# Normalizing and turning a batch's activations with ScalarE and DMA in place of VectorE and TensorE, with the first gate reordered

## The chip, the cores and the metric

The kernel runs on one core of a Trainium2 chip. The time is the device time of one execution in microseconds (us). The kernel before was timed three times ahead of the prediction: 1895.6 us in the median, 1895.07 to 1895.95.

## The reference, cut to what matters

There are 64 graphs of 256 nodes with 256 channels, in f32. One layer is applied to each:

```python
h = jnp.maximum(_layernorm(x, axis=-1), 0.0)          # "h" below, turned: channels on partitions
# inside the layer, with x = h:
xc = jnp.transpose(x, (0, 2, 1))
h = relu(bn1(conv1(xc)))                               # 256 -> 256, one tap
h = bn2(conv2(h))                                      # 256 -> 256, 17 taps
x_conv = jnp.transpose(relu(h + xc), (0, 2, 1))
s = x @ w_se.T + b_se                                  # 3 numbers per node
A = jnp.exp(-dist(s)) * mask                           # mask = adj
msg = relu(x @ w_msg.T + b_msg)
x_nmp = jnp.einsum('bnm,bmd->bnd', A, msg)
gi = concat([x_conv, x_nmp]) @ w_ih.T + b_ih           # GRU gate
gh = x @ w_hh.T + b_hh
... r, z, n as in a GRU ...
return (1.0 - z) * nn_ + z * x                         # added to the layer's input
```

## The kernel before

Two graphs make a pair (512 columns), four pairs make a block of eight graphs. There are 32 pairs and eight blocks. conv2 is done by a transform along the nodes: 16 "bins" of products with transformed weights (`wb`, read from DRAM again in each block), then back transforms on VectorE (DVE) and ScalarE (ACT). While block b is worked on, the pairs `nxt` to `nxt+3` of block b+1 are loaded, normalized, turned and put through conv1. In the trace the tiles are called `x` (a loaded pair), `hT` (turned h), `h` (conv1's result), `zT` (the three numbers for the distances), `e` (Exp of the distances), `Yv` (conv2's result), `halves` (16-bit halves, turned by DMA), `halves_d` (the same in DRAM).

In the timelines read here, the order of instructions on each engine is that of the program text. A `pace` object only postpones DVE's transform steps; `pace.flush(mark)` issues all postponed steps up to a mark.

```python
def load_x(i, eng=nc.sync):                       # SyncE's queue
    X[i] = work.tile([P, G * MC, D], FP, name="x", bufs=2)
    load_rows(X[i], x, i, eng)

def turn_adj(i):                                  # the adjacency is turned by DMA already
    HALVES[i] = late.tile([P, 2 * MC, W], U16, name="halves")
    nc.sync.dma_start_transpose(out=HALVES[i],
                                in_=adj[G * i:G * (i + 1)].rearrange("g n m -> (g n) m").bitcast(U16))

def keep_adj(i):                                  # and put away in DRAM
    ADJD[i] = dram.tile([L // 2, 2 * MC, NW, W], U16, name="halves_d", bufs=6)
    v = ADJD[i].rearrange("h q (k a) n -> k a (h q) n", a=4)
    for k in range(2 * MC):
        nc.sync.dma_start(out=v[k], in_=HALVES[i][:, k])

# norm_steps: DVE takes means and variances, GpSimd the power, then DVE scales:
def scale(j):
    nc.vector.tensor_scalar(X[i][:, j, :], X[i][:, j, :], t["mv"][:, j, 0:1], t["rstd"][:, j:j + 1],
                            ALU.subtract, ALU.mult)

def transpose_h(i):                               # eight TensorE transposes per pair
    HT[i] = work.tile([P, DC, W], FP, name="hT", bufs=6)
    for dc in range(DC):
        p = aux()
        for j in range(G * MC):
            transpose(chunk(p, j // MC, j % MC), X[i][:, j, dc * P:(dc + 1) * P])
        ...
            nc.scalar.activation(HT[i][:, dc, :], p, AF.Relu)
    if i + 2 < B // G:
        load_x(i + 2)

def gates(i, dc, wait=None, early=None):          # h, xn: early products; xc: conv2's
    ...
    product(ghn, h, n, True, True)
    nc.scalar.activation(gn, ghn, AF.Identity, ...)
    product(pr, h + xn, r, True, False)
    if early:
        early()
    product(pn, xn, n, True, False)
    product(pz, h + xn, z, True, False)
    if wait:
        wait()
    product(pr, xc, r, False, True)               # xc is Yv: conv2's result after its Relu
    nc.scalar.activation(tr, pr, AF.Tanh, ...)
    ...

# the middle of a block:
products(b, 6)                # bins 12 and 13; each bin loads the weights of the bin three later
transpose_h(nxt)
products(b, 7)                # bins 14 and 15
...
aggregate(i + 1)
message(i + 2)
conv1(nxt)
embed(i + 2)
def wait(j=0):
    pace.flush(joined[j])
gates(i, 0, wait, lambda i=i: affinity(i + 2, True))     # affinity: the distances and their Exp
load_adj(i + 3)
turn_adj(nxt)
gates(i, 1)
...
```

## Time and profile before

| | before |
|---|---|
| median of the first three runs | 1895.6 us |
| span of the profiled run | 1898.5 us |
| steady block, start to start | 221.6 us |
| TensorE's mean granted clock, as a share of the full one | 0.989 |

The prediction below shows the lines of the page and reads them; here is only how they are written. A line of a timeline has a start, a duration, an engine, a source line, an operation, `out<-in`, shapes and a count, and in brackets how long the engine stood idle just before and what released it. PE is TensorE, SPq is SyncE's DMA-issuing queue. The durations of TensorE's instructions overlap (a product of 512 columns lasts 594 ns on the page, and the next starts after 0.43 us), so a steady loss on TensorE is counted from the start of one product to the start of the next, less the usual distance of such products (0.43 us for 512 columns, 0.11 us for 128). "Stop" below means that excess at one place.

### The profile page before, as it was taken

What the parts mean: (1) busy time and instruction counts of PE and PEld (TensorE: products, weight loads), DVE (VectorE), ACT (ScalarE), POOL (GpSimd) and SP (SyncE); (2) the same over time, 40 slices, a digit from 0 to 9 for tenths busy, and PEclk for the clock granted to TensorE, in tenths of its full rate; (3) what the DMA queues carried; (4) which work ended last, traced back from release to release, by engine and by line L of the source; (5) the groups of instructions that cost most, each with busy time, mean ns of one, the idle gap of its engine ahead of it and who ended that gap; (6) DMA issues with size and microseconds to landing.
All of it is one profiled execution on the core that took longest, in us unless ns stands there. A gap on an engine that the chain in (4) does not pass through costs nothing.

```text
span 1898.5 us, 21985 instructions
## 1 busy us (share of the span) xinstructions
PE 1836.8 (97%) x7710; PEld 1141.9 (60%) x7710; DVE 1398.1 (74%) x2675; ACT 637.4 (34%) x1335; POOL 206.4 (11%) x324
## 2 busy tenths in 40 slices
PE   6899899999999999999999999999999999999997
PEld 4677445875549554694458755495546944586543
DVE  5778647996399955998379963999559983798522
ACT  2424322243313443235222433134432352224311
POOL 2110110101110110111101011101101111010000
PEclk9989999999999999999999999999999999999999
DMA  5777431672327432492316713274323923063010
GB/s 173 248 241 204 95 82 34 186 186 49 85 55 232 118 87 58 104 244 57 90 34 185 188 48 87 55 229 121 84 61 102 241 62 79 23 182 107 1 44 22
DMA packets 179071, 217.63 MB, mean 115 GB/s; under 512 B 85038, under 2 KB 104778, under 8 KB 178961
## 3 DMA queue, kind: packets, MB, share of 16 engines
q1 hardware_dynamic: 146389, 157.61, 29.1%
q0 software_dynamic: 30464, 56.73, 12.4%
q10 hardware_dynamic: 2108, 1.89, 0.3%
q8 instruction: 61, 1.00, 0.2%
q14 instruction: 49, 0.40, 0.1%
HBM read 156.54 MB, written 44.30 MB: 106 GB/s over the span
## 4 chain that ended last, share of the span: by engine, by line
PE 82%; DVE 8%; DMA 4%; issue 3%; ACT 1%; POOL 1%; ACTq 0%; POOLq 0%; SPq 0%; DVEq 0%
PE acc L479 70%; PE aux L479 8%; PE aux L483 3%; DVE Yv L59 1%; PE aux L759 1%; DMA taps<-in_c_wT_dram 1%; DVE e L766 1%; DVE Yv L62 1%; DVE T L65 1%; DVE Yv L65 1%; DMA wb<-filt 1%; DMA x<-in_x_dram 1%; DMA filt<-fo 1%; DVE msg L731 1%; DVE V L65 1%
## 5 line engine op out<-in xcount | busy, mean ns | idle before, releaser
L479 PE MATMUL acc<-hT,w_hh 128*128 128x512 f32 x768 | 354.5, 598 | 5.0 <-ACT h L618 5.0
L479 PE MATMUL acc<-xnm,w_ih 128*128 128x512 f32 x768 | 353.3, 594 | 0.0
L479 PE MATMUL acc<-Yv,w_ih 128*128 128x512 f32 x768 | 341.1, 594 | 9.5 <-ACT Yv L719 9.5
L479 PEld LDWEIGHTS acc<-Yv,w_ih 128*128 128x128 f32 x768 | 145.4, 190 | 196.0 <-issue 177.0
L479 PEld LDWEIGHTS acc<-xnm,w_ih 128*128 128x128 f32 x768 | 145.9, 191 | 183.3 <-issue 181.3
L479 PEld LDWEIGHTS acc<-hT,w_hh 128*128 128x128 f32 x768 | 144.0, 192 | 172.8 <-issue 161.6
L820 ACT ACTIVATE tr<-acc,b_rz 128x512 f32<-128x512 f32 x64 | 44.0, 687 | 541.6 <-PE acc L479 541.6
L822 DVE SCALAR_TENSOR_TENSOR gn<-tr,gn 128x512 f32<-128x512 f32 x64 | 44.2, 691 | 209.9 <-ACT tr L820 209.9
L848 POOL DMA_DIRECT2D out_dram<-y x64 | 39.0, 615 | 890.9 <-DVE y L847 861.8
L479 PE MATMUL acc<-hT,w_c 128*128 128x512 f32 x256 | 119.9, 613 | 6.4 <-ACT hT L599 5.5
L479 PE MATMUL acc<-U,wb 128*128 128x128 f32 x1024 | 124.8, 276 | 1.1 <-DMA wb<-filt 1.1
L479 PE MATMUL acc<-V,wb 128*128 128x128 f32 x1024 | 124.8, 275 | 0.0
L479 PEld LDWEIGHTS acc<-U,wb 128*128 128x128 f32 x1024 | 120.5, 192 | 5.0 <-DVE Yv L59 2.3
L59 DVE SCALAR_TENSOR_TENSOR V<-T,V 128x256 f32<-128x256 f32 (+2 forms) x224 | 121.6, 609 | 0.3
L479 PEld LDWEIGHTS acc<-V,wb 128*128 128x128 f32 x1024 | 119.5, 192 | 0.0
L479 PE MATMUL aux<-e,msg 128*128 128x256 f32 x464 | 105.0, 380 | 0.0
L479 PEld LDWEIGHTS aux<-e,msg 128*128 128x128 f32 x464 | 86.2, 191 | 11.3 <-issue 1.0
L479 PE MATMUL aux<-w_msg,hT 128*128 128x259 f32 x384 | 92.1, 390 | 0.0
L847 DVE TENSOR_TENSOR y<-aux,y 128x512 f32<-128x512 f32 x64 | 41.1, 684 | 68.4 <-PE aux L483 68.4
L523 POOL TENSOR_TENSOR rstd<-rstd,neg_half 128x4 f32<-128x4 f32 x32 | 36.3, 1134 | 497.2 <-DVE rstd L522 497.1
L65 DVE TENSOR_TENSOR V<-h 128x512 f32<-128x512 f32 x64 | 43.9, 685 | 57.9 <-ACT h L618 57.9
L479 PEld LDWEIGHTS acc<-hT,w_c 128*128 128x128 f32 x256 | 50.0, 197 | 57.7 <-issue 47.3
(148 smaller groups left out, 2737.5 us busy)
## 6 DMA issues: line engine op xcount, KB each, us to landing
wb<-filt SPq DMA_DIRECT2D x376, 256.0 KB
x<-in_x_dram SPq DMA_DIRECT2D x64, 256.0 KB
y<-in_x_dram POOLq DMA_DIRECT2D x64, 256.0 KB, 5.5
out_dram<-y POOLq DMA_DIRECT2D x64, 256.0 KB, 5.2
halves_d<-halves SPq DMA_DIRECT2D x116, 128.0 KB
adjh<-halves_d POOLq DMA_DIRECT2D x116, 128.0 KB, 5.5
filt<-fo SPq DMA_DIRECT2D x24, 252.0 KB
filt<-fo POOLq DMA_DIRECT2D x12, 252.0 KB, 5.3
```

What stands on the lines that cost most here:

```text
L59: return self.step(out, lambda: self.v.scalar_tensor_tensor(out, x, s, y, op0=ALU.mult, op1=ALU.add))
L62: return self.step(out, lambda: self.v.tensor_add(out, x, y))
L65: return self.step(out, lambda: self.v.tensor_sub(out, x, y))
L479: nc.tensor.matmul(p, w, v, **kw)
L483: nc.tensor.transpose(p, v, ident)
L523: nc.gpsimd.tensor_tensor(t["rstd"], t["rstd"], neg_half, ALU.pow)
L731: nc.vector.tensor_add(MSG[i][:, g, c, :], p[:, :D + SE], b_msg)
L759: nc.tensor.matmul(p[:, :N], ZT[rows_q, :P], ZT[rows_q, P:], start=True, stop=True)
L820: nc.scalar.activation(tr, pr, AF.Tanh, bias=b_rz[:, dc:dc + 1], scale=0.5)
L822: nc.vector.scalar_tensor_tensor(gn, tr, 1.0, gn, op0=ALU.add, op1=ALU.mult)
L847: nc.vector.tensor_add(row_tile(Y[i], g), p, row_tile(Y[i], g))
L848: nc.gpsimd.dma_start(out=rows(out, G * i + g), in_=row_tile(Y[i], g))
```

## The change

The intent is to take the transposes of h off TensorE, which is the bound, for 28 of the 32 pairs. ScalarE normalizes a pair in place (Relu with a scale and a shift), a DMA transposes its 16-bit halves from SBUF to SBUF, eight DMAs sort the rows into `hh`, and two ScalarE copies join the halves to `hT`. In the first gate of a block, the distances and conv1 of pair nxt are moved behind the early products, just ahead of the products that need conv2's result.

```diff
+    def turn_h(i):
+        for j in range(G * MC):
+            nc.scalar.activation(X[i][:, j, :], X[i][:, j, :], AF.Relu, scale=STATS[i]["rstd"][:, j:j + 1],
+                                 bias=STATS[i]["shift"][:, j:j + 1])
+        t = late.tile([P, 2 * MC, W], U16, name="halves")          # the adjacency's one buffer
+        TURNED[i] = t.rearrange("p a b -> p (a b)").rearrange("p (q n) -> p q n", n=P)
+        nc.sync.dma_start_transpose(out=TURNED[i], in_=X[i].rearrange("p q d -> p (q d)").bitcast(U16))
+        if i + 2 < B // G:
+            load_x(i + 2)
+    def sort_h(i):
+        HH[i] = late.tile([P, 2 * MC, W], U16, name="hh")
+        for j in range(2):
+            for k in range(K):
+                h = k % 2 * (P // 2)
+                nc.sync.dma_start(out=HH[i][h:h + P // 2, k // 2 * 2 + j, :], in_=TURNED[i][j::2, k::K, :])
+    def join_h(i):
+        HT[i] = work.tile([P, DC, W], FP, name="hT", bufs=6)
+        for j in range(2):
+            nc.scalar.copy(v[:, j], u[:, j])
...
-        norm(nxt)
+        turn_h(nxt)
         affinity(i + 1)
         products(b, 6)
-        transpose_h(nxt)
+        sort_h(nxt)
         products(b, 7)
-        pace.add(mix(fft.p_back(Yu, T), fft.q_factors(Yu)))
+        pace.add(mix(fft.p_back(Yu, T), fft.q_factors(Yu)), scaled)
...
         message(i + 2)
-        conv1(nxt)
-        embed(i + 2)
-        def wait(j=0):
-            pace.flush(joined[j])
-        gates(i, 0, wait, lambda i=i: affinity(i + 2, True))
+        def wait():
+            pace.flush(scaled)
+            join_h(nxt)
+            affinity(i + 2, True)
+            conv1(nxt)
+            pace.flush(joined[0])
+        gates(i, 0, wait, lambda i=i: embed(i + 2))
         load_adj(i + 3)
+        pace.flush(normed[1])
+        turn_h(nxt + 1)
+        sort_h(nxt + 1)
         turn_adj(nxt)
...
-        gates(i, 1)
         keep_adj(nxt)
+        gates(i, 1, None, lambda nxt=nxt: join_h(nxt + 1))
+        pace.flush(normed[2])
+        turn_h(nxt + 2)
+        sort_h(nxt + 2)
         turn_adj(nxt + 1)
-        transpose_h(nxt + 1)
+        keep_adj(nxt + 1)
...                                              (the same for nxt + 2 and nxt + 3 further on)
-        gates(i + 1, 0)
+        gates(i + 1, 0, None, lambda nxt=nxt: join_h(nxt + 2))
         message(i + 3)
         conv1(nxt + 2)
...                                              (y with one buffer, a "shift" per pair; join_adj moved)
```

The checks for pairs beyond the last are left out here. `K` is 4, and `u` and `v` are views of `hh` and `hT`.

More of the change, by code (lines that the diff above doesn't have):

```diff
@@ L425, in load_y @@
     def load_y(i):
-        Y[i] = late.tile([P, G * MC, D], FP, name="y", bufs=2)
+        Y[i] = late.tile([P, G * MC, D], FP, name="y")
         load_rows(Y[i], x, i, nc.gpsimd)
@@ L503, in columns @@
         return [c[:, sum(n[:j]):sum(n[:j + 1])] for j in range(len(n))]
+    STATS = {}
     def norm_steps(i):
@@ L514, in stats @@
                 t["st"] = work.tile([P, G * MC, 6], FP, name="st")
-                t["mv"] = work.tile([P, G * MC, 2], FP, name="mv")
-                t["rstd"] = work.tile([P, G * MC], FP, name="rstd")
+                t["mv"] = work.tile([P, G * MC, 2], FP, name="mv", bufs=2)
+                t["rstd"] = work.tile([P, G * MC], FP, name="rstd", bufs=2)
+                t["shift"] = work.tile([P, G * MC], FP, name="shift", bufs=2)
+                STATS[i] = t
             nc.vector.bn_stats(t["st"][:, j, :], X[i][:, j, :])
@@ L523, in aggregate_stats @@
             nc.gpsimd.tensor_tensor(t["rstd"], t["rstd"], neg_half, ALU.pow)
+            if i >= PB:
+                nc.vector.tensor_scalar(t["shift"], t["mv"][:, :, 0], -1.0, None, ALU.mult)
+                nc.gpsimd.tensor_tensor(t["shift"], t["shift"], t["rstd"], ALU.mult)
         def scale(j):
@@ L601, in transpose_h @@
             load_x(i + 2)
+    TURNED, HH = {}, {}
+    def turn_h(i):
+        if i >= B // G:
+            return
+        for j in range(G * MC):
[7 more added lines that the diff above has]
+    def sort_h(i):
+        if i >= B // G:
+            return
+        HH[i] = late.tile([P, 2 * MC, W], U16, name="hh")
+        K = D * 2 // P
+        for j in range(2):
[3 more added lines that the diff above has]
+    def join_h(i):
+        if i >= B // G:
+            return
+        HT[i] = work.tile([P, DC, W], FP, name="hT", bufs=6)
+        v = HT[i].bitcast(U16).rearrange("p c (n j) -> p j c n", j=2)
+        u = HH[i].rearrange("p (c j) n -> p j c n", j=2)
+        for j in range(2):
+            nc.scalar.copy(v[:, j], u[:, j])
     def conv1(i):
@@ L789, in aggregate @@
             nc.scalar.activation(XNM[i][:, dc, :], p, AF.Copy)
-        join_adj(i + 1)
     OT = {}
@@ L848, in finish @@
             nc.gpsimd.dma_start(out=rows(out, G * i + g), in_=row_tile(Y[i], g))
-        if i + 2 < B // G:
-            load_y(i + 2)
+        if i + 1 < B // G:
+            load_y(i + 1)
     def mix(a, b):
@@ L860, in mix @@
         return q
-    odd, even, normed, halved = (Mark() for _ in range(4))
+    odd, even, halved, scaled = (Mark() for _ in range(4))
+    normed = [Mark() for _ in range(PB)]
     joined = [Mark() for _ in range(PB)]
@@ L937 @@
         pace.flush(even)
+        run(norm_steps(nxt)[0])
         pace.add(fft.branch_back(Yv, T, 2))
@@ L940 @@
         aggregate(i)
-        if b == 0:
+        if b > 0:
+            join_adj(i + 1)
+        else:
             nc.gpsimd.dma_start(out=w_hh, in_=hh_wT.rearrange("(k p) o -> p k o", p=P))
@@ L961, in join @@
             pace.add([(W, lambda o=o: residual(i + j, o)) for o in range(DC)], joined[j])
-        stats, scale = norm_steps(nxt + 1)
         join(0)
-        pace.add(stats)
+        pace.add(norm_steps(nxt + 1)[0], normed[1])
         join(1)
-        pace.add(scale, normed)
         pace.add(split_steps(nxt), halved)
+        pace.add(norm_steps(nxt + 2)[0], normed[2])
         join(2)
@@ L973 @@
         aggregate(i + 1)
+        if b > 0:
+            join_adj(i + 2)
         message(i + 2)
-        conv1(nxt)
-        embed(i + 2)
-        def wait(j=0):
-            pace.flush(joined[j])
-        gates(i, 0, wait, lambda i=i: affinity(i + 2, True))
+        def wait():
[5 more added lines that the diff above has]
+        gates(i, 0, wait, lambda i=i: embed(i + 2))
         if b == 0:
             transpose_a(i + 2)
+            load_y(0)
         load_adj(i + 3)
+        pace.flush(normed[1])
+        turn_h(nxt + 1)
+        sort_h(nxt + 1)
         turn_adj(nxt)
-        if b == 0:
-            load_y(0)
-            load_y(1)
-        gates(i, 1)
         keep_adj(nxt)
+        gates(i, 1, None, lambda nxt=nxt: join_h(nxt + 1))
+        pace.flush(normed[2])
+        turn_h(nxt + 2)
+        sort_h(nxt + 2)
         turn_adj(nxt + 1)
-        pace.flush(normed)
-        transpose_h(nxt + 1)
+        keep_adj(nxt + 1)
         aggregate(i + 2)
+        join_adj(i + 3)
         pace.flush(halved)
         conv1(nxt + 1)
-        stats, scale = norm_steps(nxt + 2)
-        pace.add(stats)
+        pace.add(norm_steps(nxt + 3)[0], normed[3])
         pace.add(split_steps(nxt + 1), halved)
-        pace.add(scale, normed)
         pace.flush(joined[1])
-        gates(i + 1, 0)
-        keep_adj(nxt + 1)
-        turn_adj(nxt + 2)
-        pace.flush(normed)
-        transpose_h(nxt + 2)
+        gates(i + 1, 0, None, lambda nxt=nxt: join_h(nxt + 2))
         message(i + 3)
         conv1(nxt + 2)
-        stats, scale = norm_steps(nxt + 3)
-        pace.add(stats)
         pace.add(split_steps(nxt + 2), halved)
-        pace.add(scale, normed)
         finish(i)
         embed(i + 3)
+        pace.flush(normed[3])
+        turn_h(nxt + 3)
+        sort_h(nxt + 3)
+        turn_adj(nxt + 2)
+        keep_adj(nxt + 2)
         gates(i + 1, 1)
-        keep_adj(nxt + 2)
-        turn_adj(nxt + 3)
         affinity(i + 3)
         load_adj(nxt)
-        gates(i + 2, 0)
+        gates(i + 2, 0, None, lambda nxt=nxt: join_h(nxt + 3))
+        turn_adj(nxt + 3)
         keep_adj(nxt + 3)
-        pace.flush(normed)
-        transpose_h(nxt + 3)
         aggregate(i + 3)
+        join_adj(nxt)
         conv1(nxt + 3)
```

## The prediction

> **What bounds the kernel now.** I read the head of the page first, then the table of stretches (busy time per engine between given times), then the timeline of one block of eight graphs, then the waits of TensorE and of the DMA-issuing queue.
>
> ```profile
> span 1898.5 us, 21985 instructions
> PE 1836.8 (97%) x7710; PEld 1141.9 (60%) x7710; DVE 1398.1 (74%) x2675; ACT 637.4 (34%) x1335; POOL 206.4 (11%) x324
> PE   6899899999999999999999999999999999999997
> PEclk9989999999999999999999999999999999999999
> ```
>
> TensorE is busy from the third slice on, at full clock. The stretches show the same by block: the kernel is 107 us of set-up, then eight blocks; the steady ones repeat every 221.6 us.
>
> ```profile
> core 0: us, PE busy (x) PEld busy (x) DVE busy (x) ACT busy (x) POOL busy (x), PEclk, DMA share, GB/s
> 107.00:388.00 281.00, 271.50 (x1284) 181.88 (x1284) 211.65 (x409) 87.06 (x200) 28.59 (x42) 0.98 0.50 138
> 1053.00:1274.00 221.00, 219.51 (x931) 136.19 (x929) 173.07 (x332) 75.64 (x160) 23.74 (x36) 1.00 0.42 113
> 1060.00:1080.00 20.00, 20.00 (x114) 15.96 (x113) 18.47 (x35) 12.51 (x30) 2.73 (x5) 1.00 0.94 208
> 1080.00:1100.00 20.00, 18.51 (x49) 7.82 (x48) 18.78 (x40) 8.89 (x17) 3.74 (x5) 1.00 0.30 78
> ```
>
> In a steady block TensorE lacks 1.5 us of 221. Even busy time overstates the room, as instructions overlap, so I counted from start to start: the only steady loss above 0.3 us at a place is in the first gate of the block, about 3 us. DVE is nearly full (18.5 and 18.8 of 20 us) just before and in that gate, and the DMA engines are at 0.94 ahead of it. So the path is TensorE's instruction stream; what leaves that stream shortens the time, unless its replacement arrives late.
>
> ```profile
> 1061.64 1.04 PE L483 MATMUL aux<-ident,x 128*128 128x128 f32 x8
> 1062.52 1.06 PE L479 MATMUL acc<-U,wb 128*128 128x128 f32 x8
> ...
> 1082.95 0.71 PE L759 MATMUL aux<-zT 9*128 9x256 f32 x6
> 1084.11 0.69 PE L759 MATMUL aux<-zT 9*128 9x256 f32 x2 [0.46 <-ACT e L760]
> 1084.74 1.98 PE L479 MATMUL acc<-xnm,w_ih 128*128 128x512 f32 x4
> ...
> 1091.19 5.42 PE L479 MATMUL acc<-Yv,w_ih 128*128 128x512 f32 x12 [1.03 <-ACT Yv L719]
> ```
>
> The first two lines give the price of turning one pair of graphs: 1062.52 - 1061.64 = **0.88 us** for eight transposes. The distances take 1084.74 - 1082.95 = 1.8 us, most of it waiting for the fourth of them, whose PSUM buffer ScalarE's first Exp must free; then 1.2 us pass before Yv is ready.
>
> [...]one transpose lasts 273 ns but the next starts after 0.11 us, so I price by starts. [...]The write of the adjacency halves has 4 outermost[...]; the trace's 512 packets of 1 KB do take 7.4 to 10 us from issue to last packet. No run here shows a DMA transpose whose source is SBUF.
>
> ```profile
> L526 DVE TENSOR_SCALAR x<-x,mv,rstd 128x256 f32<-128x256 f32 x128 | 44.4, 409 | 44.2 <-POOL rstd L523 44.2
> L423 ACT COPY adj<-adjh 128x1024 uint16<-128x1024 uint16 x58 | 73.6, 1338 | 11.5 <-DMA adjh<-halves_d 11.5
> L599 ACT ACTIVATE hT<-aux 128x512 f32<-128x512 f32 x62 | 33.4, 592 | 8.9 <-PE aux L483 8.9
> SPq L394 <- DMA halves_d<-halves: 147.8, 41, 8.0
> ```
>
> **The change part by part.** There are 32 pairs; the first four keep the old way, 28 change (seven blocks of four).
>
> Removed from TensorE: 28 x 0.88 = **24.6 us**, all on the path. Removed from DVE: the scaling, 28 x 4 x 0.409 = 46 us, and some of the 44.2 us it waited for rstd; off the path except before the first gate, where it brings Yv about 2 us earlier (1.38 us of scaling and 0.59 us of waiting in the block that I read). Added to DVE and GpSimd: one tiny instruction each per pair.
>
> ScalarE per pair: four Relus of 256 columns with two operands[...]; two joins like the row of adj, 2.6 us; minus two of 0.59. That is +3.4 us, 95 us in all: 637 becomes about 730 of 1880, no bound by total. But it is in order, so where the work stands matters.
>
> DMA per pair: a transpose of 0.5 MB (the adjacency one, of equal size, took 3.8 to 4.0 us from issue to last packet alone, 7 us beside other loads), then eight sorting DMAs of 64 KB in 256-byte pieces (0.57 us of issue each, as for halves_d[...]: estimated 6.5 to 8 us), with a 0.5 MB load of x between them. So one pair needs about 2 + 4 + 1.3 + 7 + 2.6 = 17 us from turn_h to hT.
>
> Now the four places of a block, with TensorE's times of the block shown:
>
> 1. Pair nxt, turned in the products. The weights of the last bin are now issued behind the transpose and the x load. Before, they went out near 1057 and were used near 1065; now the queue is blocked from about 56.6 to 62.3, and they land near 65 to 66 against 64.3. Estimate **+0.8 us** (0 to 2).
>
> In the gate, distances and conv1 come after the early products. Of the old 3 us the DVE part goes. But on ScalarE the order is now: copy of zT, postponed factors, join (2.6), Exps, conv1's Relus, then Yv's Relu. The fourth distance waits for an Exp behind the join (1.5 to 2.5 us), and Yv's Relu stands behind conv1's second Relu (about 0.25 + 0.7 + 0.75 = 1.7 us after conv1's end). Together about 3.4 us in place of 3.0: **+0.4**.
>
> 2. Pair nxt+1, turned after the first gate. hT is ready about 18 us later; conv1 needs it 15.45 + 3.46 = 18.9 us later. Tight, but **0**. ScalarE then is late with tr by some 5 us, which the free PSUM buffers cover.
>
> 3. Pair nxt+2. The transpose needs the one halves buffer, behind sort, adjacency transpose (4) and its write to DRAM (7.5): it starts 25 to 27 us after the gate's end, the join ends at 38 to 43. The gate's tr is due at 34.5; DVE's queue stands behind tr, then message's additions, then the transposes of z. Up to 4 us of lateness are free; beyond, TensorE waits. Estimate **+0.5 us**, 0 to 5.
>
> 4. Pair nxt+3 has 15 us of room: **0**.
>
> Sum per block: -3.52 + 0.8 + 0.4 + 0.5 = -1.8; times seven = -12.7 us. The single y buffer costs nothing: the last y loads about 13 us after the previous output is issued, when the final addition is 16 us away. 1895.6 - 12.7 = **1883 us**.
>
> **The rivals.** (a) The transfers are hidden and the new gate order fills the old wait too: 24.6 + up to 7 x 2.9 = 45 us, 1851 us. For it: everything had 10 us or more of apparent room, and ScalarE is 66% idle. Against it: conv1's Relus stand before Yv's. (b) The chain of transfers through one halves buffer becomes the wait, in places 2 and 3, above all if the transpose from SBUF or 256-byte pieces are slower than I think: 3 to 7 us a block more, and a TensorE clock that falls after such stops (block one shows 0.98): 1905 to 1935 us. For it: the queue already waits 147.8 us for that buffer. Against it: a first use after the wait has up to 4 us of slack. (c) ScalarE's order costs the first gate more than the transposes save, DVE or ScalarE being the bound there: near 1895.
>
> **Range and chances.** I take the middle sum, 1883. My four estimates together have an uncertainty of about 3 us a block, so about 20 us, with a longer tail upwards from (b), since it repeats in seven blocks: 1852 to 1925. Faster by over 2% needs less than 1857.7, nearly all of (a): 0.10. Slower by over 2% needs more than 1933.5: 0.12. Within 2%: 0.78.
>
> **What would show it.** The transposes of x fall from 256 to 32; their 24.6 us must be gone from TensorE's starts. Step 1: TensorE waits for wb before the last bin's products, and idles before the fourth distance (released by Exp) and before Yv's products (released by its Relu). Steps 2 and 3: ScalarE's hT copies wait for the hh transfers; if TensorE then idles before conv1 or before the transposes of z, rival (b) holds. If none of these waits is in the trace, (a) does. I am wrong if the transpose from SBUF lasts far from 4 us, if the sorting lasts far from 7, or if the engines' orders are not those of the text.

## The result, and the profile after

| | before | after |
|---|---|---|
| median, runs of the same rounds | 1895.78 us (1895.07 to 1901.47, 4 runs) | **1956.37 us** (1947.74 to 1960.61, 4 runs) |
| ratio | | 1.0307, 95% interval 1.0266 to 1.0348: slower |
| span of the profiled run | 1898.5 us | 1945.9 us |
| steady blocks | 221.6 us | 229.2 to 231.8 us |

A ratio is the mean time of one kernel's runs over that of the other's of the same rounds, so it is not quite the ratio of the medians. The profiled run of the kernel after was the fastest of its four.

The first lines of the page of the kernel after:

```profile
span 1945.9 us, 22052 instructions
PE 1834.1 (94%) x7486; PEld 1129.5 (58%) x7486; DVE 1366.0 (70%) x2591; ACT 726.3 (37%) x1447; POOL 219.2 (11%) x352
...
PEclk8999999999999999999999999999999999999998
```

TensorE has 224 matmuls fewer (7710 - 7486 = 28 x 8, the transposes), yet almost the same busy time, and its share fell from 97% to 94%. ACT's 726.3 us is what the prediction had estimated ("about 730"). So the work is where the change puts it; the 47 us more of span are time in which TensorE stands, or runs slower. The table of stretches of the kernel after, for a whole steady block and for 16 us in its middle (us from the span's start, length, busy time and count of PE, PEld, DVE, ACT, POOL, then granted clock, DMA share, GB/s):

```profile
1068.00:1299.00 231.00, 219.94 (x904) 134.98 (x903) 169.31 (x322) 89.23 (x177) 25.95 (x41) 0.99 0.50 127
1084.00:1100.00 16.00, 10.59 (x78) 10.38 (x77) 8.29 (x17) 1.25 (x4) 0.00 (x0) 0.79 0.78 181
```

Where TensorE lacked 1.5 us of a steady block before, it now lacks 11, half of it in this short stretch, where its mean clock also fell to 0.79. The waits of TensorE in the kernel after (engine, output, line, whom it waited for: us in total, times, longest) name the causes:

```profile
PE acc L479 <- DMA wb<-filt: 31.8, 7, 5.4
PE acc L479 <- ACT hT L643: 14.5, 7, 3.1
PE acc L479 <- ACT Yv L761: 9.9, 7, 1.5
```

The first occurs seven times, once in each block that turns pairs: TensorE waits for weights. The second is conv1 waiting for the join of the halves. The third was there before, 9.5 us.

**The weights (place 1).** The timeline of the kernel after, in the middle of a block:

```profile
1082.77 3.28 SPq L622 DMA_TRANSPOSE halves<-x  x1
...
1087.91 1.36 SPq L377 DMA_DIRECT2D x<-in_x_dram  x2
...
1089.36 2.40 SPq L700 DMA_DIRECT2D wb<-filt  x5
...
1096.17 2.08 PE L479 MATMUL acc<-U,wb 128*128 128x128 f32 x8 [5.41 <-DMA wb<-filt]
1098.04 1.91 PE L479 MATMUL acc<-PT,wb 128*128 128x128 f32 x8
```

and the same place in the kernel before:

```profile
1057.37 3.89 SPq L658 DMA_DIRECT2D wb<-filt  x5
...
1064.05 3.66 SPq L658 DMA_DIRECT2D wb<-filt  x6
1065.19 1.06 PE L479 MATMUL acc<-U,wb 128*128 128x128 f32 x8
```

Before, the weights of the last bin went out with the five DMAs at 1057.37 and were used at 1065.19 without a wait. After, the queue issues the transpose, waits for it to end, issues the load of the next x, and only then, at 1089.36, the weights. They are used 6.8 us later, after a stop of 5.6 us. Of these 6.6 us from the transpose's issue to the weights' issue, 5.1 pass before the load of x is issued (the queue's waits are shown under place 3). In the packets of the trace, none moved for almost 2 us, from 1087.41, where the transpose's packets end, to 1089.36; then 2 KB packets start, at most eight in flight at a time until 1090.5. A packet carries neither the name of its DMA nor of its engine; that the first of them are x's follows from the order of issue. The second of the 16 products after the stop starts after 0.38 us and the others every 0.21, where they started every 0.11: 1098.04 - 1096.17 = 1.87 us for the first eight, which took 1066.09 - 1065.19 = 0.90 before. That is 1.8 us more for the sixteen. The clock that the trace records was at half from 1093.01, inside the stop, to 1099.84 (columns as above):

```profile
1093.01:1099.84 6.83, 3.67 (x17) 3.67 (x18) 0.42 (x1) 0.66 (x2) 0.00 (x0) 0.50 0.92 236
```

The block shown has the longest of the seven stops. They last 5.3, 4.5, 4.0, 4.6, 5.6, 4.8 and 4.3 us from start to start, 33 us in all, and with the slow products after them 47 us.

**The first gate.** The timeline of the kernel after:

```profile
1115.94 2.53 ACT L643 COPY hT<-hh 128x1024 uint16<-128x1024 uint16 x2
...
1118.76 0.69 PE L801 MATMUL aux<-zT 9*128 9x256 f32 x2 [0.57 <-ACT e L802]
...
1124.56 5.42 PE L479 MATMUL acc<-Yv,w_ih 128*128 128x512 f32 x12 [1.48 <-ACT Yv L761]
```

Distances (1.9 us) and the stop before Yv's products (1.64 us from start to start) make 3.5 us in place of 3.0.

**conv1 of the third pair (place 3).** The timeline of the kernel after:

```profile
1145.82 2.42 SPq L394 DMA_TRANSPOSE halves<-in_adj_dram  x1
...
1158.23 1.96 SPq L622 DMA_TRANSPOSE halves<-x  x1
...
1170.08 2.60 ACT L643 COPY hT<-hh 128x1024 uint16<-128x1024 uint16 x2 [10.28 <-DMA hh<-halves]
1170.23 1.03 PE L479 MATMUL acc<-w_msg,hT 128*128 128x259 f32 x4
...
1172.55 0.67 ACT L861 ACTIVATE tr<-acc,b_rz 128x512 f32<-128x512 f32 x1
1172.73 3.70 PE L479 MATMUL acc<-hT,w_c 128*128 128x512 f32 x8 [1.46 <-ACT hT L643]
...
1178.13 1.09 PE L483 MATMUL aux<-ident,d 128*128 128x128 f32 x8 [1.70 <-DVE msg L773]
```

and of the kernel before:

```profile
1139.48 3.59 PE L479 MATMUL acc<-hT,w_c 128*128 128x512 f32 x8
...
1142.91 1.04 PE L483 MATMUL aux<-ident,d 128*128 128x128 f32 x8
```

The h of nxt+2 could be turned only at 1158.23, because the adjacency of nxt took the one `halves` buffer at 1145.82 and then had to be written to DRAM. The waits of the DMA-issuing queue of the kernel after say so for the whole run (L622 issues the transpose of x, L377 the loads of x):

```profile
SPq L622 <- DMA halves_d<-halves: 82.2, 26, 5.6
SPq L377 <- DMA halves<-x: 56.4, 26, 3.5
```

ScalarE stood 10.28 us at the join, and the gate's tr stood behind it in ScalarE's order until 1172.55. TensorE therefore stops twice: before conv1 for hT, and after it, because DVE's message additions stand behind tr's step. From conv1 to the transposes of d it takes 5.40 us where it took 3.43.

The account of this steady block, counted from start to start against the same places before:

| place | us |
|---|---|
| transposes of four pairs gone | -3.5 |
| place 1: stop for weights 5.6, slow clock after it 1.8 | +7.4 |
| first gate | +0.6 |
| places 2 and 4 | 0 |
| place 3: before conv1 1.6, after it 2.0, transposes of d and z 1.1 | +4.7 |
| sum | +9.2 (221.6 to 230.8) |

In other blocks the split in place 3 differs: in the one ahead of it conv1 stops 3.3 us, and then each of four of its products takes 0.42 us more. The block shown is mild in this place; all seven sum to some 38 us. The block periods add up: the six steady ones are 8 to 10 us longer each (55 in all), the first is 2.5 and the last 5.6 us shorter, together the 47 us between the two profiled runs. The first block is shorter in spite of its own stops, 7.2 us at place 1 and 6.3 at place 3, because stops of the kernel before are gone from it, the longest 5.2 us at 237.53; in the last block one of 3.1 us at 1740.95 is gone. No run was made to find out why.

### The profile page after: what moved, and what is told of

The parts are those of the page before. It is cut to its first block, busy times and chain, and to the rows that moved or that the text cites. A ratio compares the mean times of both kernels' runs of the same rounds, so it can differ in the third digit from the quotient of the medians.

```text
span 1945.9 us, 22052 instructions
## 1 busy us (share of the span) xinstructions
PE 1834.1 (94%) x7486; PEld 1129.5 (58%) x7486; DVE 1366.0 (70%) x2591; ACT 726.3 (37%) x1447; POOL 219.2 (11%) x352
## 4 chain that ended last, share of the span: by engine, by line
PE 62%; DMA 14%; ACT 9%; DVE 7%; issue 4%; SPq 2%; POOL 1%; ACTq 0%; POOLq 0%; DVEq 0%
PE acc L479 54%; PE aux L479 6%; DMA halves<-x 4%; DMA x<-in_x_dram 3%; DMA wb<-filt 2%; PE aux L483 2%; ACT hT L643 2%; DMA hh<-halves 2%; ACT x L618 2%; SPq L634 1%; DMA taps<-in_c_wT_dram 1%; DVE Yv L62 1%; DVE Yv L59 1%; ACT Yv L761 1%; SPq L377 1%
## 5 line engine op out<-in xcount | busy, mean ns | idle before, releaser
L479 PE MATMUL acc<-U,wb 128*128 128x128 f32 x1024 | 131.4, 285 | 31.8 <-DMA wb<-filt 31.8
L479 PEld LDWEIGHTS acc<-U,wb 128*128 128x128 f32 x1024 | 126.1, 200 | 36.7 <-DMA wb<-filt 33.2
L479 PE MATMUL acc<-hT,w_c 128*128 128x512 f32 x256 | 126.2, 639 | 21.0 <-ACT hT L643 14.5
L643 ACT COPY hT<-hh 128x1024 uint16<-128x1024 uint16 x56 | 72.5, 1335 | 161.7 <-DMA hh<-halves 159.6
L527 POOL TENSOR_TENSOR rstd<-rstd,neg_half 128x4 f32<-128x4 f32 x32 | 40.2, 1255 | 534.7 <-DVE shift L529 498.3
L479 PEld LDWEIGHTS aux<-w_msg,hT 128*128 128x128 f32 x384 | 73.8, 194 | 18.6 <-issue 7.2
```

What stands on the lines that cost most here:

```text
L479: nc.tensor.matmul(p, w, v, **kw)
L527: nc.gpsimd.tensor_tensor(t["rstd"], t["rstd"], neg_half, ALU.pow)
L643: nc.scalar.copy(v[:, j], u[:, j])
```

## The experiments

All runs gave correct results. The kernel before, run beside each set, gave medians of 1895.14 to 1896.84 us, so the medians of the sets can be set side by side; ratios are against the before of the same rounds. By the record's verdicts, at a threshold of 2%, the change and experiments 4, 7 and 12 are slower than the kernel before, experiment 8 is unclear, and all others are the same; smaller differences rest on the 95% intervals in brackets. Diffs are against the kernel after unless the text says otherwise. There were two theories of the 60 us. The first: the queue's order (x load ahead of the weights) costs place 1. The second: the one halves buffer, shared by h and the adjacency, costs place 3. Their rivals: the amount of DMA traffic whatever its order, ScalarE's order, and the new order of the gate.

### 1. x_late_first: pair nxt's x load behind the sort

```diff
-        turn_h(nxt)
+        turn_h(nxt, False)               # no load_x in it
...
         sort_h(nxt)
+        load_x(nxt + 2)
```

> Only the pair turned in the products: its load of x is issued after the sorting DMAs, not between the transpose and the last bin's weights. Theory (the weights stand behind the x load, which itself waits for the transpose to land): TensorE's wait for the weights of the last bin, 5.6 us a block with about 1.8 us of slow clock after it, falls below 1 us; seven blocks, so about 45 to 50 us less than the changed kernel: near 1908 us. Rival (the traffic of the transpose itself saturates the DMA engines): the wait stays above 4 us and the time near 1950.

Measured: 1902.09 us (1900.72 to 1903.59), ratio 1.0038 [1.0018, 1.0058]. Two lines of its timeline:

```profile
1059.73 2.43 SPq L700 DMA_DIRECT2D wb<-filt  x5
...
1064.43 1.06 PE L479 MATMUL acc<-U,wb 128*128 128x128 f32 x8
```

The weights are now issued 4.7 us ahead of their use, and TensorE doesn't wait. Some 54 us of the 60 are gone, by moving one load (45 between the two profiled runs, where the stops and their slow products were 47). Place 3 still stops for 3 to 5 us a block. The first theory is shown for place 1; since the transpose itself stayed ahead of the weights, it is not the transpose alone but the load behind it. The load had two effects, which this run takes away together: it held up the weights' issue (6.6 us after the transpose's with it, 1059.73 - 1056.60 = 3.1 us without), and, by the order of issue, its packets went ahead of theirs (in the kernel after it is issued at 1087.91 and they at 1089.36).

### 2. x_pool_first: the same load issued by GpSimd

```diff
-        turn_h(nxt)
+        turn_h(nxt, nc.gpsimd)           # load_x(i + 2, eng)
```

> The same load of x at the same moment with the same bytes, but issued by GpSimd. Theory (order in one queue): the wait for the weights falls below 1.5 us as in x_late_first, time 1905 to 1920 us. Rival (bytes beside each other on the same DMA engines): it falls little, stays above 3.5 us, time above 1935.

Measured: 1914.05 us (1902.96 to 1918.08), ratio 1.0093 [1.0057, 1.0128]. The weights' wait, 31.8 us in all in the kernel after, is gone here too. But when GpSimd's load moved its bytes is not shown, so order and traffic are not separated by this run. In its place the distances of the first gate stop 1.87 us in place of 0.8, and in some blocks conv1 runs slower after that (the granted clock of the profiled run is 0.986). So the rival of traffic is neither shown nor ruled out; what is settled is that the load ahead in the same queue is enough to cause the wait.

### 3. adj_later: the adjacency of nxt turned after the h of nxt+2

```diff
         sort_h(nxt + 1)
-        turn_adj(nxt)
-        keep_adj(nxt)
...
         sort_h(nxt + 2)
+        turn_adj(nxt)
+        keep_adj(nxt)
```

> The adjacency transpose and write of pair nxt moved behind the turning and sorting of h of pair nxt+2, so h of nxt+2 no longer waits for them to free the one halves buffer. Theory A (halves buffer delays place three): h of nxt+2 is turned at once when normalized, about 4 us earlier; TensorE's waits around conv1 of nxt+2, 4.7 us a block, fall to 1 us; about 20 to 26 us less than the changed kernel. Theory B (ScalarE is late by itself, since the join stands early in its queue): less than 8 us.

Measured: 1923.22 us (1919.3 to 1927.74), ratio 1.0151 [1.0124, 1.0178]. The wait of conv1 for hT is gone from place 3; 0.4 to 1.2 us remain there. That is 33 us less than the kernel after, more than the 20 to 26 forecast, with the transfers unchanged in number and size. The second theory is shown as far as the place in line goes: what delayed the pair was the adjacency ahead of it. As this run takes the adjacency out of the queue and out of the buffer at once, that it is the buffer rests on the queue's wait of 82.2 us shown above. The wait for the weights is as it was, 30.5 us.

### 4. join_late: the join of nxt+2 moved behind the gate's tr on ScalarE

```diff
-        gates(i + 1, 0, None, lambda nxt=nxt: join_h(nxt + 2))
+        gates(i + 1, 0)
         message(i + 3)
+        join_h(nxt + 2)
         conv1(nxt + 2)
```

> The join of h of pair nxt+2 is moved in ScalarE's queue from early in the gate to just before its conv1. Theory A (transfer chain too long): conv1 still waits for the transfer, about 2 to 3 us a block, but the message additions and the transposes of z are no longer late (1.6 and 1.1 us a block gone): about 10 to 19 us less. Theory B (position in ScalarE's queue is the cause): all 4.7 us go, 30 us less.

Measured: 1969.07 us (1964.86 to 1969.94), ratio 1.0388 [1.0368, 1.0408]: worse than the kernel after, and outside what either theory had forecast. tr is now early, but conv1 stops 5.25 us for hT in each block, and its next products start 0.42 to 0.59 us late each. One line of TensorE's waits:

```profile
PE acc L479 <- ACT hT L643: 35.7, 7, 5.1
```

So ScalarE's order only chooses which of two stops TensorE gets; it is no cause by itself, and the place that the change gave the join was the better one.

### 5. both: experiments 1 and 3 together

> x_late_first and adj_later together. If the two causes are separate and add (43 to 50 us and about 30 us off 1954), the time is 1870 to 1882, a block 218 to 220 us, with no wait for weights and under 1.5 us around conv1 of nxt+2; what is left beyond the transposes saved is the first gate's 2.4 us a block. If place three was only late because place one had moved things (rival), it stays above 1888.

Measured: 1881.25 us (1874.2 to 1884.54), ratio 0.9914 [0.989, 0.9938]. The kernel is now faster than the one before, with steady blocks of about 220.8 us. The two gains were 54 and 33 us alone and are 75 together, so they nearly add. Of the stops above half a microsecond, the distances' 0.8 and the 1.64 us before Yv's products are left in every steady block, and single ones of 0.7 to 1.4 us at a conv1 or in place 3 in two of the six.

### 6. both_yv_first: Yv's Relu ahead of conv1

```diff
             affinity(i + 2, True)
+            pace.flush(joined[0])
             conv1(nxt)
-            pace.flush(joined[0])
```

> As both, and in the first gate the wait for Yv is put ahead of conv1 in program order, so Yv's Relu stands before conv1's Relus in ScalarE's queue. Theory (Yv's products wait because its Relu stands behind conv1's second Relu): the 1.64 us at Yv's products fall to under 0.4, 1.3 us a block, 9 to 11 us less than both. Rival (DVE's residual is late anyway): under 4 us.

Measured, on top of experiment 5: 1879.58 us (1875.57 to 1880.15), ratio 0.9906 [0.989, 0.9922], no clear difference from experiment 5. The stop before Yv's products is gone as expected, but conv1 of nxt+1 now stops 1.0 to 1.6 us for its hT: the time won was turned into a new wait, as the transfer did not become any earlier. The forecast of 9 to 11 us missed for that reason.

### 7. both_old_gate: experiment 5 with the old order of the gate

```diff
         message(i + 2)
+        join_h(nxt)
+        conv1(nxt)
+        embed(i + 2)
         def wait():
-            pace.flush(scaled)
-            join_h(nxt)
-            affinity(i + 2, True)
-            conv1(nxt)
             pace.flush(joined[0])
-        gates(i, 0, wait, lambda i=i: embed(i + 2))
+        gates(i, 0, wait, lambda i=i: affinity(i + 2, True))
```

> As both, with the old order in the first gate (conv1 ahead of the gate, distances early). Tells what the new gate order is worth. My sum says new and old order cost about the same (2.4 to 3.0 us a block): within 6 us of both. If the new order was the gain the change wanted, both is 10 us or more faster than this.

Measured: 1962.95 us (1961.37 to 1964.5), ratio 1.0352 [1.0335, 1.0369]. conv1 stops 6.28 us for pair nxt's hT, Yv's products 3.0 us, and after both the products are slow (the granted clock of the profiled run is 0.972, in experiment 5 it is 0.989). One line of TensorE's waits:

```profile
PE acc L479 <- ACT hT L643: 46.5, 11, 6.1
```

I had forecast a difference within 6 us; it is 82. Not all of it need be conv1's and the distances' order, as this edit also drops `pace.flush(scaled)` (see experiments 12 and 13): DVE stands 11.4 us for the postponed factors ahead of Yv. But in experiment 14, which keeps that line, it stands 11.0 us too, and the loss is 71 us. The new order is no addition to the change but a part that it needs: it gives pair nxt's transfer the time of the early products.

### 8. xall_adj_yv: all x loads behind their sorts, with experiments 3 and 6

```diff
         nc.sync.dma_start_transpose(...)            # turn_h
-        if i + 2 < B // G:
-            load_x(i + 2)
...
             nc.sync.dma_start(out=HH[i]...)         # sort_h
+        if i + 2 < B // G:
+            load_x(i + 2)
```

> As both_yv_first, with the load of x behind the sorting DMAs for all four pairs, not for the first alone. If the x load ahead of the sorting DMAs also holds up places two and three, another 2 to 5 us less; if those places have slack by now, within 2 us.

Measured: **1858.44 us** (1856.6 to 1862.39), ratio 0.9802 [0.9783, 0.982], the fastest of all, 21 us less than experiment 6 where 2 to 5 were forecast. The head of its page, and a steady block in the table of stretches (columns as above):

```profile
span 1854.8 us, 22049 instructions
...
1040.00:1257.00 217.00, 216.34 (x900) 132.90 (x899) 169.20 (x320) 88.51 (x176) 26.17 (x40) 1.00 0.54 134
```

A steady block takes 217.3 us, TensorE lacks 0.7 us of it, and its clock is 1.00. Only 0.8 us at the distances are left as a stop. The four transposes' 3.5 us are really won: 221.6 - 3.5 = 218.1, and the stop of 1.2 us before Yv's products, which is gone, is more than the 0.8 us that remain.

### 9. xall: the x loads alone

> The changed kernel with only the load of x moved behind the sorting DMAs, for all four pairs; adjacency and gate as in the change. If the x load was what made place three late (1.3 us of issue and about 3 us of transfer ahead of each sorting), little is left there and the time is 1870 to 1882. If the halves buffer is needed too, the waits around conv1 of nxt+2 stay at 2 to 4 us a block and the time is near 1895.

Measured: 1891.07 us (1888.78 to 1892.33), ratio 0.9969 [0.995, 0.9988]. Sorting ahead of the x loads helps nxt+2 as well: 11 us less than experiment 1. But the time is near the 1895 forecast for the case that the buffer is needed too: place 3 still stops 1.2 to 3.1 us in all in the steady blocks, with slow products after it in two of the six.

### 10. xall_yv: experiment 8 without 3 (the loads and Yv's Relu ahead of conv1)

> xall with Yv's Relu ahead of conv1's. If place three has slack, about 10 us less than xall (1.6 us a block at Yv's products); if not, the time won there is lost again at a conv1, as in both_yv_first, and it is within 4 us of xall.

Measured: 1896.61 us (1895.27 to 1901.58), ratio 1.0005 [0.9983, 1.0027]. That is 5.5 us more than experiment 9, outside both forecasts. The 1.64 us saved in the first gate come back in place 3: conv1 of nxt+2 stops 2.1 to 3.7 us in the steady blocks and then, in five of the six, runs slow (the granted clock of the profiled run is 0.986, in experiment 9 it is 0.990). With the buffer still in the way, an earlier Yv is no gain.

### 11. xall_adj: experiment 8 without 6

> xall_adj_yv without the Yv order: says what that order is worth once hT is early everywhere. Theory: the 1.64 us a block at Yv's products are back, so 9 to 13 us more than xall_adj_yv (1858). Rival (no use, as in both_yv_first): within 4 us.

Measured: 1864.2 us (1860.9 to 1868.02), ratio 0.983 [0.9807, 0.9852], with blocks of 218.7 us and the 1.64 us before Yv's products back. I had forecast 9 to 13 us more than experiment 8; it is 5.8. The stop costs what it lasts and no slow products follow it here (the granted clock of the profiled run is 0.990, as in experiment 8), and the last block gains something back (214.5 against 216.1 us). So experiment 6's step is worth something once the transfers are early.

### 12. gate_alone: the kernel before with the new order of the gate alone

Against the kernel before:

```diff
         message(i + 2)
-        conv1(nxt)
-        embed(i + 2)
-        def wait(j=0):
-            pace.flush(joined[j])
-        gates(i, 0, wait, lambda i=i: affinity(i + 2, True))
+        def wait():
+            affinity(i + 2, True)
+            conv1(nxt)
+            pace.flush(joined[0])
+        gates(i, 0, wait, lambda i=i: embed(i + 2))
```

> The kernel before with the new order of the first gate alone (distances and conv1 after the early products), h still turned by TensorE. My sum: the old 3.0 us a block at distances and Yv become 2.4 to 3.4, so within 5 us of the kernel before. Rival (the order itself is a gain of the change): 12 us or more faster.

Measured: 1950.49 us (1949.2 to 1953.64), ratio 1.0289 [1.0265, 1.0314]. The forecast missed. TensorE's waits of this kernel show where:

```profile
PE acc L479 <- ACT Yv L719: 52.9, 8, 7.2
```

I had left out the line `pace.flush(scaled)`. Without it, ScalarE's postponed factors of the back transform stand behind the Exps, DVE waits 6.6 us for them, and Yv is late. That is no verdict on the order as the change has it, so it was run again with the line.

### 13. gate_alone_flush: the same with the factors flushed first

```diff
         def wait():
+            pace.flush(scaled)
             affinity(i + 2, True)
```

> gate_alone with the flush of the postponed factors ahead of the distances. Theory (in gate_alone the factors stood behind the Exps in ScalarE's queue, so DVE waited 6.6 us a block): the wait at Yv's products falls from 7.4 to 2 to 4 us and the time to 1895 to 1912. Rival (the order itself is bad with h turned by TensorE): stays above 1930.

Measured: 1891.49 us (1888.67 to 1893.5), ratio 0.9973 [0.9949, 0.9997]. Blocks take 222.0 us against 221.6: with TensorE still turning h, the new order costs about 0.4 us a steady block; the first and the last are shorter (229.4 against 235.2 and 215.8 against 220.1 us). The time is a little under the forecast of 1895 to 1912. One flush is worth 59 us.

### 14. best_old_conv1: experiment 8 with conv1 ahead of the gate

```diff
         message(i + 2)
+        join_h(nxt)
+        conv1(nxt)
         def wait():
             pace.flush(scaled)
-            join_h(nxt)
             affinity(i + 2, True)
             pace.flush(joined[0])
-            conv1(nxt)
```

> xall_adj_yv with conv1 of pair nxt (and its join) back ahead of the gate. Theory (conv1's new place hides the transfer of pair nxt): TensorE waits 4 to 7 us a block for hT at conv1, 1895 to 1915. Rival (not needed any more): within 8 us of 1858.

Measured: 1929.48 us (1927.03 to 1933.85), ratio 1.0176 [1.0153, 1.0199]. One line of TensorE's waits:

```profile
PE acc L479 <- ACT hT L643: 42.8, 8, 6.1
```

conv1 stops 6.3 us in each block, and each of the seven starts after it is 0.30 to 0.59 us late. The 71 us of the difference from experiment 8 are this place: moving conv1 was the needed half of the new order. It came out somewhat worse than forecast: the slow products add 3 us a block there, and a stop of 1.3 us before Yv's products with slow ones after it nearly 3 more.

### 15. best_old_dist: experiment 8 with the distances at their old place

```diff
+        embed(i + 2)
         def wait():
             pace.flush(scaled)
             join_h(nxt)
-            affinity(i + 2, True)
             pace.flush(joined[0])
             conv1(nxt)
-        gates(i, 0, wait, lambda i=i: embed(i + 2))
+        gates(i, 0, wait, lambda i=i: affinity(i + 2, True))
```

> xall_adj_yv with the distances back at the early place of the gate, conv1 left at its new one. Theory (the distances' place matters little by itself: 0.7 us of wait at either place): within 6 us of 1858. Rival (they are needed to cover ScalarE's join): conv1 waits about 1.5 us a block more, 10 us or more slower.

Measured: 1891.72 us (1889.22 to 1892.8), ratio 0.997 [0.9948, 0.9993]. I had forecast "within 6 us" of experiment 8; it is 33. `embed` now stands directly behind the message whose numbers it turns, so TensorE stops 2.03 us before those transposes, some slow products follow (the granted clock of the profiled run is 0.985, in experiment 8 it is 0.990), and conv1 stops 0.8 us for hT. As the larger stop is at `embed`, which had to come ahead of the early distances, the run shows what this whole arrangement costs; an early place of the distances with `embed` elsewhere was not tried. So moving conv1 is needed (experiment 14), and the new place of the distances is at least better than this one.

### What could not be tried

A halves buffer of its own for h would settle the second theory without moving the adjacency. It does not fit: the build stops with the message that the pool of these tiles would need 58 KB per partition where 55.09 KB are left. It stays open.

## Why the prediction was wrong

It said 1883 us (1852 to 1925); the median was 1956.37, beyond the range and beyond even the rival nearest to it, (b), at 1905 to 1935.

**What held.** TensorE's stream is the path, and the 24.6 us of transposes are gone from it: experiment 8 shows the block with them removed and the new stops mended. ScalarE's load was right (726 against about 730 us), though its term for the four Relus had been an estimate that no trace had shown, and so were the durations of the single transfers: about 4.6 us from issue to last packet for the transpose in place 1 and 3.8 in place 3, 1170.08 - 1163.90 = 6.2 us from the first issue of the eight sorts in place 3 to the join, 2.08 us for the four Relus, 2.5 to 2.6 us for a join. The sorts' sum was partly luck: their issue took 5.8 us in place of 8 x 0.57 = 4.6, and the join began 0.4 us after its end, where more had been put for the landing, an estimate that no trace had shown. The gate was put at 3.4 in place of 3.0 us and measured 3.5. Places 2 and 4 cost 0, as said. One reading was loose without harm: of the distances' 1.8 us before the change, the fourth's wait is 0.8, not most.

**Step 1 failed:** "Estimate **+0.8 us** (0 to 2)" was 7.4 us. The mechanism was named rightly (weights "issued behind the transpose and the x load"), and the queue was held up only 0.9 us longer than estimated (6.6 us in place of 5.7). The mis-sized term is the weights' landing: some 3 us assumed, 6.8 us measured from issue to use, with the load of x issued just ahead of them. The 1.8 us of slow clock after the stop had no term at all. Over the seven blocks the stops and the slow products sum to 47 us where 7 x 0.8 = 5.6 was put, so this step alone is 41 us. Experiment 1 shows it from the other side with 54 us.

**Step 3 was mis-sized:** "+0.5 us, 0 to 5" was 4.7 in the block shown. The time was right: the join ended 42.9 us after the first gate's end, inside "the join ends at 38 to 43". With tr due at 34.5 that is 8.4 us late where, by the prediction, up to 4 were free. So the prediction's own figures gave 0 to 5, and I put the estimate at a tenth of that span, with no reason in the text; the late end of it was the truth. Over the seven blocks it was some 38 us in place of 3.5, so 35 us; experiment 3, which takes the cause away, won 33. The two steps together are 76 us, about what the median lies above the estimate, but the match is partly luck: the profiled run was the fastest of four, and its first and last blocks won time elsewhere.

**Where the rivals were weighed wrongly.** Rival (b) was the right one in kind for place 3, and it named the falling clock, but as a side remark of the rival and not as a term of the sum. It had nothing for place 1, which is why even its top was too low. The reading "ScalarE is 66% idle" and "10 us or more of apparent room" stood for rival (a); the idle share says nothing about an engine that stands 10.28 us at a join with tr behind it.

**What the prediction did not ask.** It priced the new order of the gate as a small cost of its own (+0.4). The number is right, but the order's worth was not seen: 71 us in experiment 14, and with the reserves named there 82 in experiment 7 and 33 in experiment 15. My forecasts of experiments 7 and 15 repeated that mistake.

## What to carry to other kernels

When work goes from the bound engine to a chain of transfers, list what stood behind it in the same queue and what shares its buffers, and price the landing of those, not only the transfer itself: here one load in front of some weights cost 54 us, and a place behind the adjacency, with one shared buffer, 33. Give a stop on the bound engine a second term for the slower products after it (here 1.8 us after one of 5.6). And place the consumers anew once the transfer is in: the same change was worth -2% or +3% by the order of a few lines.

## What the runs showed of the hardware that I had not expected

The slow clock followed surprisingly short stops, and it came late. In the trace of the kernel after, products of 128 columns started every 0.21 us in place of 0.11 after the stop of 5.6 us, and the clock was at half from 1093.01, inside the stop, to 1099.84. After the stop of 3.3 us before conv1 at 941.90, each of four products of 512 columns took 0.42 us more, and the clock was at half from 942.82, when two products had already started, to 946.23. Beyond the stop itself, the slow products cost 1.4 to 2.9 us after the seven stops of 4.0 to 5.6 us at place 1.

The length of a stop did not decide alone. In the same trace a stop of 2.7 us before conv1 at 710.06 was followed by a clock at half from 710.72 to 714.13, while stops of 2.4 and 2.1 us before conv1 at 480.13 and 1404.35 were followed by the full clock. Of four stops of 2.0 us before the transposes of d, the one before 1637.49 was followed by a clock at half from 1639.14 to 1642.55, and those before 485.53, 1178.13 and 1409.75 by the full one, as were the six of 1.64 us before Yv's products. In experiments 2, 10 and 15, stops of 1.5 to 2.1 us were in some blocks followed by three or four products that took 0.42 us more each; the granted clock of their profiled runs is 0.986, 0.986 and 0.985, where it is 0.990 in experiment 8. What else decided was not shown.

Where nothing is changed but the place of the x load, the time from the issue of the weights to their use fell from 6.8 us with a stop to 4.7 us without one. The load has 256 packets of 2 KB.

The 28 transposes from SBUF to SBUF of the kernel after, of 0.5 MB each, took 3.8 to 4.8 us from issue to the last packet, and the eight sorts of 64 KB in 256-byte rows another 6.2 us from first issue to the join in place 3.
